# A chain of attention layers: scores and values of layers 2 and 3 in eight 64x32 tiles of the array instead of four 64x64 tiles

## The chip, the core and the metric

The kernel runs on one core of a Trainium2 chip. The metric is the time of one execution on the device, in microseconds (us). The core has a matrix engine (TensorE, PE in the profile, with its weight loads shown apart as PEld), a vector engine (VectorE, DVE), a scalar engine (ScalarE, ACT), GpSimd (POOL) and a queue engine for transfers (SyncE, SP). TensorE multiplies a stationary operand, which is loaded first, with a moving one, which streams through, and writes the sums to PSUM. All data here are 32-bit floats.

## What is computed

A batch of 4 images with 64 x 64 positions and 64 channels goes through four attention layers. Layers 0, 2 and 3 are full attention over a sequence of 4096 with 64 features; layer 1 has 1024 keys of 8 features. Cut to what matters here:

```python
# layer 0: q, k, v = x W + b;  softmax(q k^T) v, times gamma, plus x
# layer 1: theta (4096 x 8), phi (1024 x 8), g (1024 x 32), the last two max-pooled
# layer 2: group norm over channels, positions are the channels of the other layout
w = jnp.einsum('bchw,bcHW->bhwHW', q, k) * scale
w = jax.nn.softmax(w.reshape(B, H, W, H * W), axis=-1).reshape(B, H, W, H, W)
out = jnp.einsum('bhwHW,bcHW->bchw', w, v)
out = linear_last(out, Wp, bp) + residual
# layer 3
h = group_norm(x, gamma, beta)
q, k, v = h @ wq + bq, h @ wk + bk, h @ wv + bv
attn = softmax(einsum('bhwc,bHWc->bhwHW', q, k) * scale)
return h + einsum('bhwHW,bHWc->bhwc', attn, v) @ wp + bp
```

## The kernel before

**Layout.** Every operand of 4096 x 64 lies as 128 partitions by 2048 columns: two halves of 64 partitions (`half(0)`, `half(1)`), each with the 64 features of half the sequence. `chunk(c)` is 512 columns, `quarter(q)` a stretch of 32 partitions. A product that reads partitions 0 to 63 uses the upper half of the array's rows, one that reads 64 to 127 the lower; the partitions of its output in PSUM set the columns of the array that it uses. So four products with 64 features and 64 output partitions each fill the array's four quadrants.

**Attention of layers 2 and 3 (`attention`, from L1272).** For one image there are 128 units: 4 chunks of queries (c) by 32 blocks of keys (j). `first(u)` (L1283) makes the scores of a unit: four products at L1288, 64 stationary key columns each, against 512 queries, into a PSUM tile `s` of 128 x 1024 (two banks; the lower half of the array writes the other bank). ScalarE takes the exponential at L1293 into a tile `p`, and VectorE adds the tiles up at L1299 (`zacc`), for the sums of the softmax. `then(u)` (L1315) makes the values, two steps later: four products at L1323, 64 stationary columns of v against `p`, accumulated over the 32 blocks in two PSUM banks, one for each half of the array's rows. After the last block the two banks are added, divided by the row sums (`sums`, L1242 on TensorE and L1247 on VectorE), and projected (`last`, L1467 in layer 2).

**Layer 0 and layer 1.** Layer 0 has the same form with its own lines (scores L999, exponential L1009, values L1028). Layer 1 runs as background work: L1075 makes theta for the first two chunks, with 64 rows and 32 columns of the array for each product, which is eight tiles; L1122 makes scores of 8 features in tiles of 32 rows and 64 columns; L1148 values in tiles of 128 rows and 32 columns.

**The order of the work.** It is written out by hand, not planned by a scheduler. `step` issues two units' scores, then two units' value products that are due (`due`), and at fixed places in between (MID, LATE, END) one piece of the background, which is a generator that yields where it may be interrupted. `later` holds vector work that is put after the value products, `urgent` the row sums and projections of chunks that are complete. When a LATE piece is ready, `parts` (L846) splits the second unit's value products in two halves of 256 columns and puts the piece in between. The background of layers 2 and 3 is the next images' normalisation and projections: L891 (queries), L912 (values), L1354 (means), L1419 and L1439 (layer 2's queries, keys, values), L1092 and L1194 (layer 1). All engines run their instructions in this order and wait for each other by semaphores.

**The order of the layers** is at the end of `fast_path` (L1774 to L1832): image 0 and the first layers of image 1, then layer 2 of one image alternates with layer 0 of the next, with layer 1 in the background; at the end come layers 3 of images 0 and 1, layer 2 of image 3, and layers 3 of images 2 and 3. So each of the eight runs of `attention` fills its TensorE time with its own 128 units and with what the background brings.

**Loads.** A product is preceded by the load of its stationary operand. In the profile each product of 32-bit floats appears as two MATMUL and two LDWEIGHTS records: 8 runs of 128 units with 4 score products are 4096 products, and L1288 has 8192 records of each kind.

A second path (`general_path`) runs only if a sum of exponentials leaves the range of the numbers; with these inputs it does not run.

Of the kernel before, what the change touches and what calls it, by code (L numbers as in the profile page):

```python
# [597 lines left out]
def fast_path(tc: tile.TileContext, a: dict, out: bass.AP, bad, read_flag):  # L598
# [11 lines left out]
    B, H, W, C = x.shape  # L610
    N = H * W
    P = 128
# [21 lines left out]
    half = lambda i: slice(i * C, (i + 1) * C)  # L634
    quarter = lambda q: slice(q * 32, q * 32 + 32)
    chunk = lambda c: ds(c * 512, 512)
# [160 lines left out]
    def ready(place):  # L797
        at = back["at"]
        if place == LATE and back["alone"] == now[0]:
            return False  # L800
        return back["credit"] >= 1.0 and (at == place or place == MID and at == ALONE)

    def urgent_now():
        return urgent and urgent[0][0] <= now[0]
# [11 lines left out]
    def step(first=None):  # L816
        back["credit"] = min(back["credit"] + back["tempo"], 3.0)
        for f in before.pop(now[0], ()):
            f()
        if first is not None:  # L820
            first()
        work = due.pop(now[0], [])
        for n, f in enumerate(work[:2]):
            if n == 1:
                advance(MID)
            split = n == 1 and ready(LATE)
            f(lambda: advance(LATE)) if split else f()
        for f in work[2:]:
            f()
        if len(work) < 2:  # L830
            advance(MID)
            advance(LATE)
        passes = list(later)
        later.clear()
        for f in passes:
            f()
        advance(END)
        now[0] += 1
# [7 lines left out]
    def parts(within, whole):  # L846

        if within is None or whole:
            yield slice(0, 512)
            if within is not None:  # L850
                within()
        else:
            yield slice(0, 256)
            within()
            yield slice(256, 512)
# [401 lines left out]
    def turn(o, zsums, spread):  # L1257


        t = o_tile("turned") if spread is None else p_tile()[:, 0:512]  # L1260
        r = sums(zsums)[1]
        nc.vector.transpose(t, o)
        if spread is None:
            divide(blocked(t), t, r)
            return t
        u = o_tile("turned")
        split = lambda t: t.rearrange("p (j n f) -> p j n f", n=2, f=32)
        r = r.rearrange("p (j n) -> p j n", n=2).unsqueeze(3).to_broadcast([P, 8, 2, 32])
        nc.vector.tensor_tensor(u.rearrange("p (n j f) -> p j n f", n=2, f=32), split(t), r, ALU.mult)
        return spread(u)  # L1270

    def attention(st, last, not_before, name, final=None, spread=None):  # L1272

        q, k, v = st.pop("q"), st.pop("k"), st.pop("v")
        ps, accs, zaccs, zsums, os = {}, {}, {}, {}, {}  # L1280
        pairs = NC * NB // 2

        def first(u):  # L1283
            c, j = divmod(u, NB)
            s = s_tile()
            for i in range(2):
                for e in range(2):
                    nc.tensor.matmul(  # L1288
                        s[half(e), chunk(i)], k[(j + i) % 2][half(i), ds(j // 2 * P + e * C, C)], q[half(i), chunk(c)],
                        start=True, stop=True,  # L1290
                    )
            p = ps[u] = p_tile()
            nc.scalar.activation(p, s, AF.Exp)  # L1293
            if j == 1:
                zaccs[c] = z_p.tile([P, 1024], FP, tag="zacc", name="zacc")
            if j >= 1:

                p0 = ps[u - 1] if j == 1 else zaccs[c]
                add = lambda: nc.vector.tensor_tensor(zaccs[c], p0, p, ALU.add)  # L1299
                later.append(add) if j % 2 or urgent_now() or ready(MID) else add()  # L1300
            if j == NB - 1:
                later.append(lambda: turn_blocks(c))

        def turn_blocks(c):

            t = p_tile()
            nc.vector.transpose(t, zaccs.pop(c))

            def sum_blocks():
                zsums[c] = small.tile([P, 32], FP, tag="zsums", name="zsums")  # L1310
                nc.vector.tensor_reduce(zsums[c], t.rearrange("p (n k) -> p n k", k=32), AX.X, ALU.add)

            later.append(sum_blocks)

        def then(u, within=None):  # L1315
            c, j = divmod(u, NB)
            if j == 0:
                accs[c] = [acc_tile() for _ in range(2)]
            p = ps.pop(u)
            for cols in parts(within, j in (0, NB - 1)):  # L1320
                for e in range(2):
                    for i in range(2):
                        nc.tensor.matmul(  # L1323
                            accs[c][e][half(i), cols], v[half(e), j, :], p[half(e), chunk(i)][:, cols],
                            start=(j == 0), stop=(j == NB - 1),
                        )
            if c == NC - 1 and j == NB - 1 and final is not None:
                final(accs.pop(c), zsums.pop(c))
            elif j == NB - 1:
                o = os[c] = o_tile("o")  # L1330
                acc = accs.pop(c)
                nc.scalar.copy(o, acc[0])
                nc.vector.tensor_tensor(o, o, acc[1], ALU.add)
                urgent.append((now[0] + 2, lambda: os.update({c: turn(os[c], zsums.pop(c), spread)})))
                end = now[0] + (4 if spread is None else 6)
                urgent.append((end, lambda: last(c, os.pop(c))))
                if c == NC - 1:
                    urgent.append((end, lambda: st.update({name: True})))

        start = now[0]  # L1340
        for t in range(pairs):
            g = max(start + t + 2, not_before + t // 2)
            due.setdefault(g, []).extend([lambda *within, u=u: then(u, *within) for u in (2 * t, 2 * t + 1)])
        for t in range(pairs):
            step(lambda: (first(2 * t), first(2 * t + 1)))
        return 0
# [541 lines left out]
```

## Time and profile before

| | us |
|---|---|
| median of 3 runs | 2927.6 (2926.52 to 2927.66) |
| profiled execution, span | 2927.0 |
| PE busy | 2895.3 |
| PEld busy | 1113.6 |
| VectorE busy | 1871.5 |
| ScalarE busy | 1800.3 |
| value products of layers 2 and 3, L1323, busy | 1006.6 |
| mean granted TensorE clock | 0.998 of full |

The span is that of one profiled execution, from its first to its last instruction; the times are those of runs without a profile. A busy time is the time in which an engine has at least one instruction under way: products that run side by side in different tiles count once, and their ends are modelled, so a row's mean of 590 ns is longer than the distance between successive groups. A row of a view names the line, the engine, the operation, the output and what it is made from, the part of the array in rows*columns, partitions x elements, and how many.

### The profile page before, as it was taken

What the parts mean: (1) busy time and instruction counts of PE and PEld (TensorE: products, weight loads), DVE (VectorE), ACT (ScalarE), POOL (GpSimd) and SP (SyncE); (2) the same over time, 40 slices, a digit from 0 to 9 for tenths busy, and PEclk for the clock granted to TensorE, in tenths of its full rate; (3) what the DMA queues carried; (4) which work ended last, traced back from release to release, by engine and by line L of the source; (5) the groups of instructions that cost most, each with busy time, mean ns of one, the idle gap of its engine ahead of it and who ended that gap; (6) DMA issues with size and microseconds to landing.
All of it is one profiled execution on the core that took longest, in us unless ns stands there. A gap on an engine that the chain in (4) does not pass through costs nothing.

```text
span 2927.0 us, 66546 instructions
## 1 busy us (share of the span) xinstructions
PE 2895.3 (99%) x29397; PEld 1113.6 (38%) x29397; DVE 1871.5 (64%) x2141; ACT 1800.3 (62%) x2481; POOL 35.2 (1%) x35
## 2 busy tenths in 40 slices
PE   9999999999999999999999999999999999999998
PEld 3333233333444433344443343333344444443333
DVE  2111753589821078963027897888888877878878
ACT  5666666665566766566766655555555655555554
POOL 0000000000000000000000000000000000000000
PEclk9999999999999999999999999999999999999999
DMA  2010000000001000000000000000000000000000
GB/s 38 1 30 7 1 1 16 7 5 5 19 5 30 1 7 5 5 23 16 1 1 7 5 9 19 19 5 9 5 19 8 20 5 8 6 20 5 8 5 10
DMA packets 85513, 30.64 MB, mean 10 GB/s; under 512 B 79168, under 2 KB 83264, under 8 KB 83808
## 3 DMA queue, kind: packets, MB, share of 16 engines
q1 hardware_dynamic: 83168, 25.87, 4.8%
q8 instruction: 232, 3.80, 0.6%
q10 hardware_dynamic: 1984, 0.38, 0.1%
q14 instruction: 65, 0.53, 0.1%
q0 software_dynamic: 64, 0.07, 0.0%
HBM read 4.79 MB, written 4.19 MB: 3 GB/s over the span
## 4 chain that ended last, share of the span: by engine, by line
PE 97%; DVE 1%; ACT 1%; issue 0%; DMA 0%; POOL 0%; ACTq 0%; DVEq 0%
PE acc L1323 30%; PE s L1288 30%; PE s L999 15%; PE acc L1028 15%; PE s L1122 2%; PE acc L1148 2%; ACT p L1128 1%; DVE zacc L1299 1%; PE s L1148 1%; PE s L891 0%; PE s L912 0%; PE s L1419 0%; PE s L1467 0%; PE s L1092 0%; PE s L1194 0%
## 5 line engine op out<-in xcount | busy, mean ns | idle before, releaser
L1293 ACT ACTIVATE p<-s 128x1024 f32<-128x1024 f32 x1024 | 994.6, 1022 | 696.2 <-PE s L1288 676.5
L1299 DVE TENSOR_TENSOR zacc<-zacc,p 128x1024 f32<-128x1024 f32 x960 | 1174.2, 1223 | 179.7 <-ACT p L1293 114.8
L1323 PE MATMUL acc<-p,v 64*64 64x512 f32 (+1 forms) x8576 | 1006.6, 573 | 0.0
L1009 ACT ACTIVATE p<-s 128x1024 f32<-128x1024 f32 x480 | 487.3, 1020 | 114.8 <-PE s L999 114.6
L1323 PEld LDWEIGHTS acc<-p,v 64*64 64x64 f32 x8576 | 340.4, 133 | 545.1 <-issue 545.1
L1028 PE MATMUL acc<-p,vs 64*64 64x512 f32 (+1 forms) x4224 | 501.4, 577 | 0.0
L1288 PE MATMUL s<-q,k 64*64 64x512 f32 x2048 | 491.6, 590 | 2.1 <-ACT p L1128 2.1
L999 PE MATMUL s<-xT,q 64*64 64x512 f32 x2048 | 487.2, 591 | 2.4 <-DVE mean L1355 0.7
L1288 PE MATMUL s<-q,xT 64*64 64x512 f32 x2048 | 489.5, 591 | 0.0
L999 PE MATMUL s<-xT,q_swapped 64*64 64x512 f32 x2048 | 487.6, 591 | 0.3 <-DVE o L1157 0.3
L1288 PE MATMUL s<-q,h_swapped 64*64 64x512 f32 x2048 | 481.0, 591 | 3.9 <-DVE v L916 3.5
L1288 PE MATMUL s<-q,k_swapped 64*64 64x512 f32 x2048 | 480.4, 590 | 0.0
L1011 DVE TENSOR_REDUCE all_z<-z 128x1 f32<-128x4 f32 x128 | 20.1, 157 | 606.5 <-ACT p L1009 606.2
L1028 PEld LDWEIGHTS acc<-p,vs 64*64 64x64 f32 x4224 | 173.3, 133 | 266.0 <-issue 264.2
L1288 PEld LDWEIGHTS s<-q,h_swapped 64*64 64x64 f32 x2048 | 145.5, 133 | 144.5 <-issue 131.7
L1288 PEld LDWEIGHTS s<-q,k_swapped 64*64 64x64 f32 x2048 | 148.1, 133 | 137.6 <-issue 87.2
L999 PEld LDWEIGHTS s<-xT,q_swapped 64*64 64x64 f32 x2048 | 146.2, 133 | 141.8 <-issue 110.3
L1288 PEld LDWEIGHTS s<-q,xT 64*64 64x64 f32 x2048 | 145.7, 133 | 138.1 <-issue 131.7
L999 PEld LDWEIGHTS s<-xT,q 64*64 64x64 f32 x2048 | 144.2, 133 | 139.3 <-issue 110.8
L1288 PEld LDWEIGHTS s<-q,k 64*64 64x64 f32 x2048 | 148.6, 133 | 116.7 <-issue 96.2
L1017 ACT ACTIVATE vs<-v,all_r 128x64 f32<-128x64 f32 x256 | 89.1, 348 | 157.2 <-PE acc L1028 80.3
L1128 ACT ACTIVATE p<-s 128x1024 f32<-128x1024 f32 x128 | 124.1, 1022 | 82.4 <-PE s L1122 78.5
(213 smaller groups left out, 1319.6 us busy)
## 6 DMA issues: line engine op xcount, KB each, us to landing
k_swapped<-k SPq DMA_DIRECT2D x8, 512.0 KB, 5.8
residual<-turned SPq DMA_DIRECT2D x128, 32.0 KB, 1.9
h_swapped<-xT SPq DMA_DIRECT2D x8, 512.0 KB, 5.3
out_dram<-turned SPq DMA_DIRECT2D x60, 64.0 KB, 2.0
xin<-in_x_dram SPq DMA_DIRECT2D x12, 256.0 KB, 6.8
q_swapped<-q SPq DMA_DIRECT2D x6, 512.0 KB, 5.5
pg<-pg SPq DMA_DIRECT2D x8, 128.0 KB, 2.3
xin<-in_x_dram SPq DMA_DIRECT2D x12, 64.0 KB, 2.4
```

Source lines behind the costliest of these rows:

```text
L999: nc.tensor.matmul(s[half(e), chunk(i)], queries(m, i, e), k[half(i), chunk(c)], start=True, stop=True)
L1009: nc.scalar.activation(p, s, AF.Exp, accum_out=z)
L1011: nc.vector.tensor_reduce(zsum[:, m : m + 1], zs.pop(m), AX.X, ALU.add)
L1017: nc.scalar.activation(vs, v[:, m, :], AF.Copy, scale=rz[:, m : m + 1])
L1028: nc.tensor.matmul(acc[c][half(i), cols], scaled[t][half(e), :], ps[NC * m + c][half(e), chunk(i)][:, cols], start=(m == 0 and not second) ...
L1122: nc.tensor.matmul(ss[e][half(m), chunk(i)], pgs[0 if e == d else 1][r, ds(n * P + m * C, C)], th[r, chunk(i ^ j)], start=True, stop=True,)
L1128: nc.scalar.activation(pk[e], ss[e], AF.Exp)
L1148: nc.tensor.matmul(acc[quarter(q), :], g[:, k, :], ps[j, k][q // 2][:, chunk(q % 2)], start=(k == 0 or not bank), stop=(k == NK - 1 or not ...
L1288: nc.tensor.matmul(s[half(e), chunk(i)], k[(j + i) % 2][half(i), ds(j // 2 * P + e * C, C)], q[half(i), chunk(c)], start=True, stop=True,)
L1293: nc.scalar.activation(p, s, AF.Exp)
L1299: add = lambda: nc.vector.tensor_tensor(zaccs[c], p0, p, ALU.add)
L1323: nc.tensor.matmul(accs[c][e][half(i), cols], v[half(e), j, :], p[half(e), chunk(i)][:, cols], start=(j == 0), stop=(j == NB - 1),)
```

## The change

Each score product of 64 stationary columns becomes two of 32, and so does each value product. The output of a product covers 32 partitions (`quarter(n)`) instead of 64. The order of the loops changes as well: the column tile is the outer loop, the half of the array's rows the inner one. Which operands are multiplied, which PSUM banks are written, and what is issued around the products stay as they are.

```diff
         def first(u):
             c, j = divmod(u, NB)
             s = s_tile()
-            for i in range(2):
-                for e in range(2):
+            for n in range(4):
+                for i in range(2):
                     nc.tensor.matmul(
-                        s[half(e), chunk(i)], k[(j + i) % 2][half(i), ds(j // 2 * P + e * C, C)], q[half(i), chunk(c)],
+                        s[quarter(n), chunk(i)], k[(j + i) % 2][half(i), ds(j // 2 * P + n * 32, 32)], q[half(i), chunk(c)],
                         start=True, stop=True,
                     )
...
             for cols in parts(within, j in (0, NB - 1)):
-                for e in range(2):
-                    for i in range(2):
+                for n in range(4):
+                    for e in range(2):
                         nc.tensor.matmul(
-                            accs[c][e][half(i), cols], v[half(e), j, :], p[half(e), chunk(i)][:, cols],
+                            accs[c][e][quarter(n), cols], v[half(e), j, ds(n % 2 * 32, 32)], p[half(e), chunk(n // 2)][:, cols],
                             start=(j == 0), stop=(j == NB - 1),
                         )
```

## Prediction

> **What bounds the kernel now.** I read the page's busy times and its chain first: which engine carries the end, and on which lines.
>
> ```profile
> span 2927.0 us, 66546 instructions
> PE 2895.3 (99%) x29397; PEld 1113.6 (38%) x29397; DVE 1871.5 (64%) x2141; ACT 1800.3 (62%) x2481; POOL 35.2 (1%) x35
> PE 97%; DVE 1%; ACT 1%; issue 0%; DMA 0%; POOL 0%; ACTq 0%; DVEq 0%
> ```
>
> TensorE is the chain: 97% of the span, while VectorE and ScalarE have a third of theirs free. In the chain by line, L1323 and L1288, the two lines that change, have 30% each. The waits of PE (the view of waits, for PE alone) are small; their two longest are:
>
> ```profile
> PE s L1148 <- ACT p L1128: 8.4, 15, 0.6
> PE s L1288 <- DVE v L916: 3.5, 1, 3.5
> ```
>
> So there is no idle time of PE to win, and whatever is added on PE is added to the end. "Busy" is not "at its peak", so next comes the timeline of PE in a stretch of layer 3 without background work (columns: start, length, engine, line, operation, count).
>
> ```profile
> 2007.35 1.89 PE L1323 MATMUL acc<-p,v 64*64 64x512 f32 x16
> 2009.07 0.59 PE L1288 MATMUL s<-q,xT 64*64 64x512 f32 x2
> 2009.08 0.59 PE L1288 MATMUL s<-q,h_swapped 64*64 64x512 f32 x2
> ...
> 2010.79 1.89 PE L1323 MATMUL acc<-p,v 64*64 64x512 f32 x16
> ```
>
> From L1323 to the next L1323 is 2010.79 - 2007.35 = 3.44 us. In it lie 32 records: two units with 4 score products and 4 value products each, every product as two records. Four records run side by side, one per 64x64 tile, so 3.44 us is 8 groups of four, 0.429 us each. All four quadrants of the array are in use in every group. Eight 64x32 tiles cover the same array once, each still streams 512 columns: a group of eight should last what a group of four does. So the change cannot win array time; the question is what it costs.
>
> **Part 1: twice the instructions.** L1288 has 4 x 2048 = 8192 matmul records and L1323 8576; after the change they are 33,536 instead of 16,768, with as many more weight loads. Groups stay 2048 + 1952 of 512 columns and 192 of 256 (7808 / 4 and 768 / 4). Needed: 8 loads and 8 matmuls in 429 ns, 26.8 ns an instruction. Does PE get them that fast? The nearest row is a projection with short products, L912, 64 matmuls and 64 loads in one go:
>
> ```profile
> 1781.21 1.07 PE L1323 MATMUL acc<-p,v 64*64 64x512 f32 x8
> 1782.07 1.14 PE L912 MATMUL s<-wv,xT 64*64 64x64 f32 x64
> 1783.00 1.07 PE L1323 MATMUL acc<-p,v 64*64 64x512 f32 x8
> ```
>
> 128 instructions in 0.93 us, 7.3 ns each. For a longer stretch I counted PE's records in the trace: the densest 10 us has 424 (23.6 ns each), the densest 20 us has 642 (31.2 ns), and neither is bounded by the supply as far as it shows. [...] By the row, 0.93 us for 64 matmuls is 14.5 ns each[...]. I take the row: 0 us[...]. Instruction fetch doubles with the counts, to cover with DMA engines that the page shows at 0 to 2 tenths busy.
>
> The loads are hidden: 133 ns under 429 ns now, and a 64x32 load takes 103 (L1075's median is 104). They come cheap only while PE can look ahead to them; without that cover the first matmul after a load is some 24 ns longer (L1075: 613 at most, 589 at least).
>
> **Part 2: switches of tile shape.** Now the attention stages of layers 2 and 3 and nearly all background work between their products have one shape, 64x64. After the change the attention has 64x32 and the background still 64x64. The trace has one row in exactly this form: L1075, layer 1's theta, four times, eight 64x32 tiles between 64x64 products.
>
> ```profile
> 544.56 1.07 PE L1323 MATMUL acc<-p,v 64*64 64x512 f32 x8
> 545.56 1.09 PE L1075 MATMUL s<-xT,wth 64*32 64x512 f32 x16
> 546.58 1.09 PE L1323 MATMUL acc<-p,v 64*64 64x512 f32 x8
> 547.49 0.60 PE L1288 MATMUL s<-q,k 64*64 64x512 f32 x2
> ```
>
> Each block is two groups, 0.858 us if they ran through. From start to start they take 1.00, 1.02 and 0.91 us: 0.14 lost at the way in, 0.16 at the way out, 0.05 until the loads are hidden again, 0.35 us for the trip. The other three trips give 0.32, 0.35 and 0.35 by the same subtraction. Start by start: after the last 512-column record the next shape begins 519 ns later, where 429 would do, at both edges and in every one of the trips. And for a group of eight itself: its second pass follows 454 ns after its first, 25 more than 429, which is the exposed first load; the matmuls start 6.7 ns apart, 54 ns for eight. So eight full streams side by side cost no array time.
>
> Short background work does not switch now and is nearly free:
>
> ```profile
> 2027.95 1.03 PE L1323 MATMUL acc<-p,v 64*64 64x512 f32 x8
> 2028.81 0.25 PE L1242 MATMUL s<-zsums,lanes 64*64 64x16 f32 x8
> 2028.90 1.06 PE L1323 MATMUL acc<-p,v 64*64 64x512 f32 x8
> ```
>
> 0.09 us. With a switch on both sides the same three terms apply (wait for the last of eight, load exposed, wait for the last short one), so I take 0.31 to 0.33 on top for L1242, L1467, L912 and L1354 too. Bounds: 0.09 (one drain, the rest hidden) and 0.52 (the whole 519 ns unhidden).
>
> How many trips? In the order of PE's instructions in the changed program there are 118 stretches of 64x64 with 64x32 on the edges: the row sums of L1242 29, L1467 14, L891 12, L912 12, L1354 10, L1028 of layer 0's last values 9, L1092, L1176 and L1194 6 each, L999 4, L1419 4, L1439 2, and four that hold several lines. Four such trips exist today (L1075), so 114 are new. Layer 1's score and value blocks (L1122, L1148) switch today as well: leaving from eight tiles costs 27 ns more spread (47 ns from the first start to the last, against 20), coming back 27 ns less exposed load (51 for a 64x64 load, 640 - 589, against 24). Nothing there.
>
> What hides a switch? Nothing: PE waits for nothing else. Behind a background product wait its reader on VectorE or ScalarE (L1247, L1473, L916), which have room, and the next scores; these are late by the same 0.3 us, and so is all that follows on PE.
>
> **The sum.** 114 trips x 0.335 us (middle of 0.32 and 0.35) = 38.2 us. Against the profiled span 2927.0 this gives 2965.2; the median of the three times, 2927.6, stands 0.6 us above the span, so **2966 us**. With 0.25 to 0.43 us a trip the sum is 28 to 49 us: 2956 to 2977.
>
> **Rivals.** The bound of what this measurement can tell from no change is 0.2%, 5.9 us.
>
> *A. The stream of eight does not hold 429 ns.* The trace has eight tiles for two groups at most, never a third; what follows is another shape. [...] a load is exposed in each pair: 25 ns x 2096 pairs = 52 us, 3018 with the trips; if each pair ends like a switch, 0.16 x 2096 = 335 us, 3300. For it: nothing in the trace shows it sustained. Against it: 6.7 ns from start to start, and loads that go ahead as soon as their tile's matmul has begun.
>
> *B. Instructions come too slowly*[...]. The 7.3 and 23.6 ns speak against it.
>
> *C. Not slower: the switch costs nothing here.* What was read at L1075 would belong to its semaphore (it waits for its tile from ScalarE), not to its shape. Then the trips are free: 2928. It decides once a trip costs under 5.9 / 114 = 0.05 us. Against it: the way back to L1323 waits for no semaphore and costs 0.16.
>
> *D. Faster.* Shorter loads and independent columns would close the small leftovers: were a group 427 instead of 429 ns, 4000 x 2 ns = 8 us, which needs the trips at nothing too: 2920. No row speaks for it.
>
> **How the numbers follow.** The trips as read 0.77, A 0.14, B 0.03, C 0.04, D 0.02. The likeliest gives 2966. Of the range, 2950 to 3035 takes the likeliest case and the cheap end of A, and leaves out C, D, B and most of A, near 2 in 10. Faster 0.02, same 0.04, slower 0.94.
>
> **What would show it.** Right: L1288 and L1323 as 64*32 with 33,536 records; 3.44 us from L1323 to L1323 in a stretch of layer 3 without background; about 1.0 us from the last value block to a 64x64 block behind it and 519 ns from last to next start at each edge; loss only at edges; the granted clock still 9 tenths throughout. Wrong: a period above 3.44 us in quiet stretches (A if matmul starts are uneven by tile, B if PE's sequencer is what they wait for), or L1242 blocks that still cost 0.09 us (C).

## The result and the profile after

The changed kernel takes 2960.75 us (median of 4, 2958.78 to 2960.88) against 2927.11 us before (median of 4): 33.6 us more, a ratio of 1.0112 with a 95% interval of 1.0098 to 1.0127. Its profiled execution has a span of 2957.1 us and is the fastest of the four; the one of before has 2927.0.

The page of the changed kernel, its busy times and its chain:

```profile
span 2957.1 us, 100082 instructions
PE 2926.4 (99%) x46165; PEld 1056.4 (36%) x46165; DVE 1873.4 (63%) x2141; ACT 1798.7 (61%) x2481; POOL 35.2 (1%) x35
PE 98%; ACT 1%; DVE 1%; issue 0%; POOL 0%; DVEq 0%
PE acc L1323 30%; PE s L1288 30%; PE s L999 15%; PE acc L1028 15%; PE s L1122 2%; PE acc L1148 2%; ACT p L1128 1%; PE s L912 1%; PE s L1148 1%; PE s L891 1%; PE s L1419 0%; PE s L1467 0%; PE s L1092 0%; PE s L1194 0%; PE s L1242 0%
```

PE has 46,165 matmuls for 29,397, as many more as counted, and stays the chain. Its busy time is 31 us longer; VectorE and ScalarE have moved by less than 2 us. The stretch without background, from the timeline of PE:

```profile
2020.03 1.92 PE L1323 MATMUL acc<-p,v 64*32 64x512 f32 x32
...
2023.46 1.92 PE L1323 MATMUL acc<-p,v 64*32 64x512 f32 x32
```

3.43 us from L1323 to L1323, with 64 records in place of 32: before it was 3.44. Eight tiles hold the pace. Where 64x64 work lies in between they do not; the same view at a projection of layer 1 (L1194) and at row sums (L1242):

```profile
700.03 1.06 PE L1323 MATMUL acc<-p,v 64*32 64x512 f32 x16
701.03 1.09 PE L1194 MATMUL s<-o,wo 64*64 64x512 f32 x8
702.05 1.09 PE L1323 MATMUL acc<-p,v 64*32 64x512 f32 x16
702.93 0.59 PE L1288 MATMUL s<-q,k 64*32 64x512 f32 x1
...
2047.50 1.06 PE L1323 MATMUL acc<-p,v 64*32 64x512 f32 x16
2048.49 0.30 PE L1242 MATMUL s<-zsums,lanes 64*64 64x16 f32 x8
2048.73 1.09 PE L1323 MATMUL acc<-p,v 64*32 64x512 f32 x16
2049.61 0.59 PE L1288 MATMUL s<-q,xT 64*32 64x512 f32 x1
```

Three blocks of 0.858 us take 1.00, 1.02 and 0.88: 0.33 us for the trip over L1194. L1242 and the two value blocks take 2.11 us, up to the score product behind them. Before, they began at 2027.95, and that score product stood here:

```profile
2029.79 0.59 PE L1288 MATMUL s<-q,xT 64*64 64x512 f32 x2
```

That is 1.84 us: 0.27 us for the trip.

Edge by edge, from the last start in the old shape to the first in the new: into 64x64, 117 of the 118 edges take 519 or 520 ns, as foretold. Back to 64x32 it depends on what the 64x64 product streamed: all 43 behind 512 columns take 519 or 520 ns, 199 ns behind 128 columns, 136 behind the 16 of L1242 (in the run with the scores alone, below, 306 behind 256). A stream of 512 columns lasts 429 ns, so at 0.838 ns a column an edge adds 90 to 92 ns behind 512, 256 and 128 columns alike. A long trip is then two such waits, the starts of the products side by side (eight are spread over 47 ns, four over 20), and the exposed first loads (51 and 24 ns): 322 ns.

To see where all of it went I used that both kernels end the same 1946 ScalarE activations in the same order. How much later a given one ends is the time lost so far. I took the growth of this lag over each step (two units, about 3.4 us) of layers 2 and 3 and grouped the steps by the background line that lies in them:

| background in the step | steps | lag gained, us each | sum, us |
|---|---|---|---|
| none | 345 | -0.006 | -2.0 |
| L1242 | 29 | 0.275 | 8.0 |
| L1467 | 14 | 0.305 | 4.3 |
| L891 | 12 | 0.332 | 4.0 |
| L912 | 11 | 0.510 | 5.6 |
| L1354 | 10 | 0.275 | 2.8 |
| L1028 | 9 | 0.322 | 2.9 |
| L1092, L1194 | 12 | 0.322 | 3.9 |
| L1176 | 6 | 0.278 | 1.7 |
| L1419, L1439 | 6 | 0.319 | 1.9 |
| L1122 with L1148 | 45 | 0.015 | 0.7 |
| L1075 | 3 | -0.331 | -1.0 |

The steps with L1075 gain because the trip that the kernel before made there is gone. The mean of L912 is not typical: most of its steps take 0.32, and three, at 753, 757 and 1251 us of the kernel before, take 0.93, 1.15 and 0.66.

The sum is 32.7 us; about 2.4 come back outside these steps, in the stages of layer 0 and between stages, which makes 30.3 us at the last activation of the two profiled executions. The -2.0 of the quiet steps is not a gain of eight tiles: nearly all of it is in the steps around 1790 us, where the kernel before ran at half clock for 6.8 us (last section).

### The profile page after: what moved, and what is told of

It is laid out like the page before. It is cut to its first block, busy times and chain, and to the rows that moved or that the text cites. A ratio compares the mean times of both kernels' runs of the same rounds, so it can differ in the third digit from the quotient of the medians.

```text
span 2957.1 us, 100082 instructions
## 1 busy us (share of the span) xinstructions
PE 2926.4 (99%) x46165; PEld 1056.4 (36%) x46165; DVE 1873.4 (63%) x2141; ACT 1798.7 (61%) x2481; POOL 35.2 (1%) x35
## 3 DMA queue, kind: packets, MB, share of 16 engines
q8 instruction: 363, 5.95, 0.8%
## 4 chain that ended last, share of the span: by engine, by line
PE 98%; ACT 1%; DVE 1%; issue 0%; POOL 0%; DVEq 0%
PE acc L1323 30%; PE s L1288 30%; PE s L999 15%; PE acc L1028 15%; PE s L1122 2%; PE acc L1148 2%; ACT p L1128 1%; PE s L912 1%; PE s L1148 1%; PE s L891 1%; PE s L1419 0%; PE s L1467 0%; PE s L1092 0%; PE s L1194 0%; PE s L1242 0%
## 5 line engine op out<-in xcount | busy, mean ns | idle before, releaser
L1323 PE MATMUL acc<-p,v 64*32 64x512 f32 (+1 forms) x17152 | 1021.1, 572 | 0.4 <-issue 0.4
L1323 PEld LDWEIGHTS acc<-p,v 64*32 64x32 f32 x17152 | 311.2, 107 | 577.3 <-issue 575.4
L1028 PE MATMUL acc<-p,vs 64*64 64x512 f32 (+1 forms) x4224 | 501.6, 578 | 0.0
L1288 PE MATMUL s<-q,k 64*32 64x512 f32 x4096 | 494.4, 590 | 2.1 <-ACT p L1128 2.1
L1288 PE MATMUL s<-q,xT 64*32 64x512 f32 x4096 | 492.6, 589 | 0.0
L1288 PE MATMUL s<-q,h_swapped 64*32 64x512 f32 x4096 | 489.2, 589 | 3.1 <-DVE v L916 3.1
L1288 PE MATMUL s<-q,k_swapped 64*32 64x512 f32 x4096 | 490.2, 590 | 0.0
L999 PE MATMUL s<-xT,q 64*64 64x512 f32 x2048 | 487.2, 591 | 2.5 <-DVE v L916 0.8
L999 PE MATMUL s<-xT,q_swapped 64*64 64x512 f32 x2048 | 488.0, 591 | 0.3 <-DVE o L1157 0.3
L1028 PEld LDWEIGHTS acc<-p,vs 64*64 64x64 f32 x4224 | 171.4, 133 | 269.5 <-issue 267.8
L1288 PEld LDWEIGHTS s<-q,h_swapped 64*32 64x32 f32 x4096 | 150.4, 107 | 144.4 <-issue 132.6
L1288 PEld LDWEIGHTS s<-q,xT 64*32 64x32 f32 x4096 | 150.2, 107 | 140.6 <-issue 134.4
L1288 PEld LDWEIGHTS s<-q,k_swapped 64*32 64x32 f32 x4096 | 147.8, 107 | 142.0 <-issue 98.0
L999 PEld LDWEIGHTS s<-xT,q_swapped 64*64 64x64 f32 x2048 | 145.8, 133 | 141.7 <-issue 110.3
L1288 PEld LDWEIGHTS s<-q,k 64*32 64x32 f32 x4096 | 147.7, 107 | 128.3 <-issue 101.6
L999 PEld LDWEIGHTS s<-xT,q 64*64 64x64 f32 x2048 | 142.8, 133 | 141.2 <-issue 107.8
```

The lines of the kernel that those rows point to most:

```text
L999: nc.tensor.matmul(s[half(e), chunk(i)], queries(m, i, e), k[half(i), chunk(c)], start=True, stop=True)
L1028: nc.tensor.matmul(acc[c][half(i), cols], scaled[t][half(e), :], ps[NC * m + c][half(e), chunk(i)][:, cols], start=(m == 0 and not second) ...
L1288: nc.tensor.matmul(s[quarter(n), chunk(i)], k[(j + i) % 2][half(i), ds(j // 2 * P + n * 32, 32)], q[half(i), chunk(c)], start=True, stop=True,
L1323: nc.tensor.matmul(accs[c][e][quarter(n), cols], v[half(e), j, ds(n % 2 * 32, 32)], p[half(e), chunk(n // 2)][:, cols], start=(j == 0), st ...
```

## The experiments

Theory S: PE loses the time at the edges between tile shapes, 0.32 us for a trip out and back (0.28 around short products). Rival G: a group of eight tiles is a little longer than one of four. Rival N: each further instruction costs a little. All times are medians against the kernel before on the same chip, 2926.6 to 2926.9 us.

**Half of the change, many more edges: only the scores.** L1288 as in the change, L1323 as before.

```diff
-            for i in range(2):
-                for e in range(2):
+            for n in range(4):
+                for i in range(2):
                     nc.tensor.matmul(
-                        s[half(e), chunk(i)], k[(j + i) % 2][half(i), ds(j // 2 * P + e * C, C)], q[half(i), chunk(c)],
+                        s[quarter(n), chunk(i)], k[(j + i) % 2][half(i), ds(j // 2 * P + n * 32, 32)], q[half(i), chunk(c)],
```

> Only the score products (L1288) in eight 64x32 tiles, the value products left at 64x64. Half of the change, but every step now goes from one shape to the other and back: the order of PE's instructions has 513 trips between 64x64 and 64x32 where the kernel before has 4. Theory S (the loss is the switches, 0.32 us a trip as read in the changed kernel's trace): 509 x 0.32 = 163 us, 3090 us. Rival G (a group of eight tiles is longer than a group of four, 33.6 us over 4192 groups = 8 ns each): half of the groups, 17 us, 2944 us. Rival N (each further instruction costs about 1 ns): the same, 2944 us.

Measured: 3087.57 us, ratio 1.055 (1.0529 to 1.0571): 160.7 us for half of the change, where the whole costs 33.6. Over 509 new trips that is 0.316 us each. The timeline of PE in this run:

```profile
2100.11 1.95 PE L1323 MATMUL acc<-p,v 64*64 64x512 f32 x16
...
2103.87 1.95 PE L1323 MATMUL acc<-p,v 64*64 64x512 f32 x16
```

The period of a quiet step is 3.76 us instead of 3.44. In the steps without background the lag grows by 0.322 us in the median, one trip in each. G and N, which expected 2944, fall as explanations of the loss.

**The other half: only the values.** The same for L1323, with L1288 as before.

```diff
-                for e in range(2):
-                    for i in range(2):
+                for n in range(4):
+                    for e in range(2):
                         nc.tensor.matmul(
-                            accs[c][e][half(i), cols], v[half(e), j, :], p[half(e), chunk(i)][:, cols],
+                            accs[c][e][quarter(n), cols], v[half(e), j, ds(n % 2 * 32, 32)], p[half(e), chunk(n // 2)][:, cols],
```

> Only the value products (L1323) in eight 64x32 tiles, the scores at 64x64: 606 trips in the order of PE's instructions against 4. Theory S with 0.316 us a trip (160.7 us for 509 trips, as the run with the scores alone measured): 602 x 0.316 = 190 us, 3117 us. Rivals G and N, half of the change: 2944 us.

Measured: 3112.64 us, ratio 1.0636 (1.0616 to 1.0655), 186 us more for 602 trips: 0.309 us each. The difference to the run before it is the background, which lies between value products: a step with L1194 in it now has two trips, 0.643 us of lag, a quiet one 0.322.

**The loops in the old order.** Eight tiles, but the half of the rows as the outer loop, in both places.

```diff
-            for n in range(4):
-                for i in range(2):
+            for i in range(2):
+                for n in range(4):
...
-                for n in range(4):
-                    for e in range(2):
+                for e in range(2):
+                    for n in range(4):
```

> The changed kernel with the loops in the order of the kernel before (the half of the array's rows outside, the column tiles inside): the tile's width without the new order. Theory S: the trips are the same, 2961 us. If the order of the tiles had its part in the loss (two halves of rows alternating in their PSUM banks): below 2955 us.

Measured: 2959.34 us (2958.03 to 2960.24), ratio 1.011 (1.0093 to 1.0127). The time is that of the changed kernel, and by steps the gains are too (0.322 at L1467, 0.274 at L1242). The order has no part in it; the width of the tile does it.

**All edges taken away but layer 1's: one shape.** The background products and layer 0 also as pairs of 64x32.

```diff
+    def narrow(out, w, rhs, start, stop):
+
+        for h in range(2):
+            nc.tensor.matmul(out[h * 32 : h * 32 + 32], w[:, h * 32 : h * 32 + 32], rhs, start=start, stop=stop)
...
-                    nc.tensor.matmul(
+                    narrow(
                         bank[i][half(e), :], w[half(i), half(e)],
```

(the last two lines at L891, and in the same way at L912, L999, L1028, L1092, L1176, L1194, L1242, L1354, L1419, L1439 and L1467)

> The changed kernel, and all other products of 64 columns (layer 0's scores and values, projections, sums, L1092, L1176, L1194 and the rest) also as pairs of 64x32, so that nothing is left to switch to but layer 1's own two shapes. Theory S: the 114 trips are gone, and with them the 4 of L1075 in the kernel before (1.4 us): 2925 to 2928 us, the same as the kernel before within 0.2%, with more instructions than any kernel yet. Rival G: layer 0's groups are longer too, 1.5 x 33.6 = 50 us, 2977 us. Rival N: the same 2977 us.

Measured: 2954.28 us, ratio 1.0096 (1.0079 to 1.0113). All three missed. The trips are gone as expected: the steps with L1028, L1092, L1194 and L1439 now gain 0.000 to 0.001 us, quiet ones 0.004 at eight tiles. But there is a new loss, in jumps of up to 4 us at the 16 places where L912 stands. From the waits of PE, then its timeline at the first of these places (all split products stand on the helper's line, 849):

```profile
PE s L849 <- issue: 11.8, 9, 3.6
...
19.40 1.20 PE L849 MATMUL s<-wv,xT 64*32 64x64 f32 x91 [0.45 <-issue]
22.90 0.76 PE L849 MATMUL s<-wv,xT 64*32 64x64 f32 x35 [2.29 <-issue]
```

L912 is a run of 64 matmuls and 64 loads, 128 of each once split. After 91 matmuls PE stands still for 2.29 us and waits for nothing that this view shows. The steps of layers 2 and 3 with L912 in them gain 1.2 us each (13 us), and layer 0's steps gain 12 us, nearly all of it next to L912. What PE waits for there comes out in the run with 128 columns, below.

**The same without that line.** L912 stays at 64x64, the rest as in the one-shape run.

```diff
-                        narrow(
+                        nc.tensor.matmul(
                             s[half(e), ds(i * 512 + k * C, C)], rhs[half(i), ds((g * 8 + k) * P + e * C, C)],
```

> The one-shape kernel, but with the short value projection L912 left as 64 products of 64x64 in a row (it is issued 16 times). The trace of the one-shape run shows all its loss at those 16 places: 128 loads and 128 matmuls at once, and pauses of PE up to 3.6 us with nothing to wait for. Theory S with a limit of instruction supply at bursts: the 16 bursts are as short as before and cost a switch each, 16 x 0.32 = 5 us: 2930 to 2933 us. If the loss of the one-shape run was anything that comes with more instructions or with eight tiles in layer 0 (rivals G and N): 2950 us or more.

Measured: 2937.93 us (2935.56 to 2940.93), ratio 1.0036 (1.0022 to 1.005). 16.4 us come back, so the split L912 was most of the new loss, and G and N, which wanted 2950 or more, fall a second time: this kernel has all of its large products in eight tiles, layer 0's too, and its quiet steps are as long as before to the nanosecond (0.000 us over 345). It is still 5 us above the expectation. What I had left out is the price of splitting the short products: 0.086 us for L1242, 0.066 for L1467, 0.1 for L1354 and L1176, 5.0 us in all; L912 costs 0.39 with its switch, 4.3 us in 11 steps.

**Some of the edges: only the short products.** The changed kernel with L1242, L1354 and L1176 through the same helper.

```diff
-                nc.tensor.matmul(
+                narrow(
                     s[half(i), ds(k * 512, 16)], both_lanes[half(k), :], zsums[half(k), i * 16 : i * 16 + 16],
```

> The changed kernel with three short background products (L1242, L1354, L1176, 1 to 32 columns) as pairs of 64x32, the rest of the background still 64x64. That takes 45 of the 114 trips away. Theory S, with 0.28 us for a short trip as read in the changed kernel's trace: 45 x 0.28 = 12.6 us less than 2960.8, 2948 us. Were a switch dear only around long products, which drain longer: 2961 us. Rivals G and N: 2961 us.

Measured: 2954.31 us (2952.36 to 2955.76), ratio 1.0096 (1.0079 to 1.0113): 6.4 us less than the changed kernel, half of what was expected. By steps, L1242 falls from 0.275 to 0.080, L1354 from 0.275 to 0.087, L1176 from 0.278 to 0.100: the switch goes, the split stays. And where such products stand in layer 0's stages, which keep 64x64, the split makes new edges, some 0.26 us each at six places. The direction is S's, the size is not: the expectation had taken the split as free.

**How many instructions are too many.** The changed kernel with its score products cut along the moving side, into two of 256 columns, then four of 128.

```diff
+            for m in range(2):
+                for n in range(4):
+                    for i in range(2):
+                        nc.tensor.matmul(
+                            s[quarter(n), ds(i * 512 + m * 256, 256)],
+                            k[(j + i) % 2][half(i), ds(j // 2 * P + n * 32, 32)], q[half(i), ds(c * 512 + m * 256, 256)],
```

> The changed kernel with each score product cut again, into two of 256 moving columns: 32 loads and 32 matmuls where the kernel before has 8 and 8, 13.4 ns an instruction in the score half of the time. Theory S: no new switch; each group of 512 becomes two of 216 (2.5 ns more than 429 for the pair), 2048 x 2.5 = 5 us: 2966 us. Rival N (1 ns for each of 32,768 further instructions): 2994 us. If PE's instructions cannot come at 13.4 ns: from 3000 us on, without a bound.

Measured: 2967.58 us (2966.88 to 2968.16), ratio 1.0138 (1.0123 to 1.0154), 7 us more than the changed kernel for 32,768 more instructions. As S had it.

> The same with four score products of 128 moving columns: 6.7 ns an instruction in the score half, just under the 7.3 ns of the densest stretch that the trace of before shows (L912). Theory S with hidden loads: four groups of 109 to 112 ns for one of 429, 7 to 19 ns more on 2048: 2975 to 3000 us. If the loads no longer hide (103 ns against a group of 107), 25 ns on 8192 groups: about 3165 us.

Measured: 3523.55 us, ratio 1.2038 (1.2016 to 1.206). Far above both expectations. The waits of PE in this run:

```profile
PE s L1289 <- issue: 193.3, 351, 3.2
PE acc L1325 <- issue: 90.6, 104, 3.6
```

PE stands still, and "issue" says that no cause is visible. Busy time by window, 40 us in layer 3, in the run with 128 columns and then in the one with 256 (columns: PE, PEld, DVE, ACT, POOL, with the number of records):

```profile
2400.00:2440.00 40.00, 34.27 (x1327) 23.37 (x1310) 23.79 (x21) 16.55 (x17) 0.00 (x0) 1.00 0.02 5
```

```profile
2000.00:2040.00 40.00, 40.00 (x1136) 22.70 (x1128) 32.78 (x30) 21.83 (x23) 0.00 (x0) 1.00 0.06 10
```

With 128 columns 2637 instructions pass in 40 us, 15.2 ns each, and PE has gaps; with 256 it is 17.7 ns each and PE has none. The pages have a row for the transfers of instructions (number, MB, share of the DMA engines). From the kernel before, the changed one, the run with 256 columns and the one with 128:

```profile
q8 instruction: 232, 3.80, 0.6%
q8 instruction: 363, 5.95, 0.8%
q8 instruction: 491, 8.04, 1.1%
q8 instruction: 747, 12.24, 1.4%
```

From 256 to 128 columns there are 65,536 more loads and matmuls and 256 more transfers: one transfer of 16.4 KB is 256 of PE's instructions, 64 bytes apiece. I counted PE's loads and matmuls between pauses of more than 0.6 us: in the run with 128 columns there are 429 such pauses, and 358 of the 428 distances between them are a multiple of 256 within two. The trace has each transfer's time as well. With 128 columns they start 3.8 us apart in the median and never under 3.1, though each takes only about 1.0: 3.8 us for 256 is 15 ns each. All 363 of PE's waits for "issue" of over 0.3 us that follow a transfer end between 1.1 and 1.75 us after one has landed, 1.4 in the median. So in this run the instructions arrive in packets of 256, and on long stretches no faster than about 15 ns each.

The short stops at the split L912 are the same shortage. Their distances are not multiples of 256, but in the one-shape run all seven such waits that follow a transfer, the 2.29 us and the longest of 3.6 us among them, end 1.3 to 1.5 us after one has landed. The same holds for a wait of 0.4 us in the first of the changed kernel's three dear steps with L912; the extra in the other two was not traced.

**A version that beats both.** The one long wait of PE in the kernel before is 3.5 us at the end of layer 2 of image 2, with a stretch of half clock behind it. Two pauses are taken out of the background in `before3`, and nothing else:

```diff
-        yield MID
         nc.vector.tensor_tensor(sums, stat[:, 0:1], stat[:, 1:2], ALU.add)
         yield MID
         summed(mean, avg3, sums)
...
-        yield MID
         sums = col("sums3")
```

> The kernel before with two pauses fewer in the background of layer 3 (the two places ahead of a one-column addition in before3), so that layer 3's value projection L912 of image 0 is issued between the last steps of layer 2 and not all at once at its end. It aims at the one long wait of PE, 3.7 us at 1785 us in the trace of before, and the half clock that the trace shows for 6.8 us behind it (3 us lost). If both go: 2920 to 2922 us. If the wait goes and the half clock is not its consequence: 2923 to 2924. If the vector engine is late anyway: 2927.

Measured: 2922.68 us (median of 21, 2920.89 to 2923.39) against 2926.76 (median of 25): ratio 0.9986, 0.9979 to 0.9992. The waits of PE:

```profile
PE s L1148 <- ACT p L1128: 8.4, 15, 0.6
PE s L1288 <- ACT p L1128: 2.1, 6, 0.6
```

The wait for L916 is gone from the list, and no stretch of half clock is left before the end of the kernel. It is 4.1 us faster than the kernel before, by this alone. That falls between the two ranges expected, with and without the half clock; the wait and the half clock had been read as 6.5 us together. Against the six executions of the kernel before that show a granted clock of 0.999, and so no half clock (last section), it is 2.2 us: the wait of 3.5 us brought less than its length, and where the rest went was not traced.

**Both together.** One shape and the two pauses fewer.

> All products of 64 columns as pairs of 64x32, as in the one-shape run, and the two pauses fewer. If the two add up: 2919 to 2922 us. If the wait at the end of layer 2 has another cause than the place of the projection: the same as the one-shape run.

Measured: 2955.22 us (2954.33 to 2956.31), ratio 1.0096 (1.008 to 1.0111), no better than the one-shape run. That run had lost most of this wait already (1.4 us left of it), and the jumps at the split L912 stay.

## Why the prediction was right, point by point

- *PE is the bound and everything added is added to the end.* Right in the main: 98% of the chain after, and a quiet step leaves the lag as it is (0.000 us in the median). By PE's own starts the quiet steps away from 1790 us give back 1.9 us in all.
- *A group of eight lasts what a group of four does.* Right: 3.43 us for 3.44, and 0.000 us over 345 quiet steps in the run that has all large products in eight tiles.
- *Instructions at 26.8 ns come fast enough, by the row of L912 (7.3 ns in a burst).* Right: 26.8 ns came without a gap in the quiet stretches (3.43 us a step), and 17.7 ns an instruction still fits. But the row that was taken could not tell: its 128 instructions fit into one transfer of 256, so a burst is no measure for a long stretch. There the limit lay near 15 ns, and the margin was a factor of 1.8 and not 3.7. As far as it rests on that row, this was luck; the 23.6 ns over 10 us was the better ground. Instruction fetch did not double either: all of PE's instructions grew by 1.57, and the transfers with them, from 3.80 to 5.95 MB.
- *Loads are hidden.* Right; a load of 64x32 takes 107 ns in the mean, under 429.
- *A trip costs 0.32 to 0.35, middle 0.335.* A little too high: 0.322 for long background, 0.275 for L1242, L1354 and L1176, for which 0.31 to 0.33 was stated and 0.335 put into the sum. Three of the four trips of L1075 gave 0.35 because the four products ahead of them started over 49 ns; the fourth, with 20 ns as all 64x64 groups around the changed kernel's edges have, gave 0.32. The way back from a short product is the 136 ns shown above and not 519: L1242 adds 0.396 us to its step, where it added 0.116 before.
- *114 new trips; layer 1's shapes cost nothing more.* Right: 0.015 us for each of 45.
- *38.2 us.* Measured 33.6. The mis-sized term is the cost of a trip: 45 short ones at 0.275 where 0.335 was put, 2.7 us too much, and 69 long ones at 0.322, 0.9 us too much. The 1 us left is no more than what the two profiled executions differ by before the first changed product (0.9 us), and was not taken apart. The half clock has no part in the 33.6; of the two profiled executions only that of before has it, and they are 30 us apart (last section).
- *Rivals.* A (the stream of eight does not hold 429 ns) fell: there is no unevenness in the quiet stretches. At 2028.2 us eight matmuls start 6 or 7 ns apart, a load starts 1 or 2 ns behind each of them, and the next eight follow 429 ns after the first. B (supply) fell at 26.8 ns an instruction, and came true near 15. C (the switch is free) fell: L1242 costs 0.28 us more than it did. D fell with it.

## What to carry to other kernels

Count a kernel's tile shapes in the order in which TensorE runs them: here every change of shape and back cost 0.3 us, which 114 times is 1.1% and 509 times 5.5%, while the number of tiles that fill the array was free (3.43 us for a step that took 3.44). A new shape pays only if it takes over everything between its products or gains more than its edges cost; making the rest follow was no way out here, since splitting the short products cost part of what it saved, and at the split L912 PE stood still for up to 3.6 us until a transfer of instructions had landed. Splitting products was free here only as long as the instructions came: some 27 ns apart was fine, 18 still fine, about 15 the limit.

## What the runs showed that I had not expected

*Instructions in packets of 256.* See the run with 128 columns: pauses up to 3.6 us, 84% of their distances a multiple of 256 instructions, and each wait for "issue" ends shortly after a transfer has landed.

*A wait of 3.5 us cost twice.* In the kernel before, PE waits at the end of layer 2 for the vector engine, which has two additions and a transpose ahead of the one that frees the tile. The timeline of PE there:

```profile
1785.22 0.62 PE L1288 MATMUL s<-q,xT 64*64 64x512 f32 x2
1785.26 0.59 PE L1288 MATMUL s<-q,h_swapped 64*64 64x512 f32 x2
1789.39 1.12 PE L1288 MATMUL s<-q,h_swapped 64*64 64x512 f32 x2 [3.53 <-DVE v L916]
1789.40 1.12 PE L1288 MATMUL s<-q,xT 64*64 64x512 f32 x2
1790.30 1.06 PE L1288 MATMUL s<-q,h_swapped 64*64 64x512 f32 x2
```

From 1788.4 to 1795.3 us the granted clock is 0.5; the records are twice as long and the groups 0.85 us apart, which costs 3 us behind a wait of 3.5. In the other profiled executions such stretches last 3.4 or 6.8 us. Of the pauses between matmul starts, all five of 3.9 us and more are followed by one (4.12 us here). Of the seven from there down to 3.4 us three are; four are not, of 3.46, 3.65 (the changed kernel), 3.66 and 3.82 us. Of the shorter ones, 3.27 us was followed by one, and so were the pauses of 2.5 us some 20 us after the start in the two runs with L912 split; 2.69 and 2.75 us were not. So at these lengths it came or did not, which makes some 2 us between executions; what decides it was not shown. Every profiled execution with a granted clock of 0.998 or less has such a stretch before its end, and every one with 0.999 has none. By this, three of the four executions of the changed kernel had it (0.998; 2960.7 to 2960.9 us) and only the profiled one did not (0.999; 2958.8), while the kernel before shows 0.998 in its profiled execution and in 19 of 25 others: the medians compare like with like. All 21 executions of the version with two pauses fewer show 0.999.
